# Two sigmoid recurrences cut into five chains of 26 rows instead of four of 32

## The chip, the cores and the metric

The kernel runs on one core of a Trainium2 chip. The metric is device time in microseconds (us) of one execution. A core has five engines that each work through their own queue of instructions in order and meet at semaphores: TensorE (PE in the profile, with PEld for its weight loads), VectorE (DVE), ScalarE (ACT), GpSimd (POOL) and SyncE (SP), which here issues the DMA transfers.

## The reference

The input `x` has shape (4, 32, 128, 128). Two layers follow each other; each is a convolution block with a residual, then a feed-forward block with a residual. The feed-forward block is what the change touches, and it stands in the program twice (`f0` after the first convolution block, `f1` at the end):

```python
def _L0_ffn_ref(x, W, V, gamma, beta):
    Wx = jnp.einsum('bti,hi->bth', x, W)
    # normalised over the whole batch, per feature
    Wx = ((flat - mean) * rsqrt(var + BN_EPS) * gamma + beta).reshape(B, T, H)
    def step(yt, wx_t):
        yt = sigmoid(wx_t + yt @ V.T)
        return (yt, yt)
    _, ys = scan(step, zeros((B, H)), swapaxes(Wx, 0, 1))
    return swapaxes(ys, 0, 1)
```

The scan runs over 4096 tokens (32 images of 128 rows) for each of 4 batch entries, and each step needs the one before it. A step is one 128 x 128 matrix product, an add and a sigmoid over 128 features.

## The kernel before

**How the recurrence is made parallel.** A sigmoid step shrinks differences fast, so the kernel doesn't start at the first token. It cuts the long scan into many short ones: each starts from a guess of 0.5 and takes `WARM = 12` steps on the tokens ahead of its own before its results count. The 128 columns of one step are the 4 batch entries times the 32 images, which run side by side; the 128 rows of an image are split among `QS = 4` chains of `LEN = 32` rows. One pass over all chains, one row each, is called a round here. So a recurrence is 12 warm-up rounds and then 32 rounds whose results count, 44 rounds of 4 steps. At the end `check` compares what each chain started from with what the chain before it ended with (tolerance `TOL`), and a flag `redo` starts a slow sequential version of everything if they differ.

**One step** (`step`, L1907 to L1913) is three instructions on three engines: a matmul of the weights with the chain's last state into a PSUM bank (L1910, two weight loads and two matmul passes in the trace[...]), on VectorE the scaled input row added in place in that bank (L1911, a SCALAR_TENSOR_TENSOR of 128x128), and on ScalarE the sigmoid from the bank into SBUF (L1912). Each chain has its own PSUM bank, with one buffer. The chains don't depend on each other, so while one is on VectorE another can be on TensorE.

**First recurrence** (`f0.scan()`, L1971). The sigmoid writes its result over the input row in `WX`. Nothing else runs on these engines meanwhile. After it come the 32 images of the second convolution block in an order written out by hand (`CONVOLUTIONS`, L54), which ends by filling `WX` and the statistics for the second recurrence; `f0.check()` is one piece of that list (`CK`).

**Second recurrence** (`f1.scan(output)`, L2252). While it warms up, SyncE's DMAs bring the residual rows back from DRAM into `XA`, turned so that partitions hold tokens (L2230). In the counting rounds, `output(i, ys)` (L2237) is called after each round for the row before: four transposes on TensorE into one PSUM bank `ps_out` (L2244, `ps_t` has two buffers), one VectorE add of that bank and `XA` into `res` (L2245, 128x512), and every second row four DMAs of `res` to the output (L2249), issued by SyncE.

**What sets the order.** The order of instructions on each engine is fixed when the kernel is built, and queues run in order. In the built program, a counting round of the second recurrence has four steps with the four transposes among them on TensorE, four adds L1911 and then the add L2245 on VectorE, and four sigmoids on ScalarE. After the last row VectorE runs `check` (L1953 to L1958), TensorE and VectorE make the flag (L2258 to L2262), all engines read it (L2289) and the program ends.

Of the kernel before, what the change touches and what calls it, by code (L numbers as in the profile page):

```python
# [40 lines left out]
GAIN = float(np.float32(np.sqrt(2.0)))  # L41


LEN, WARM = 32, 12
QS = P // LEN
TOL = 4e-6

FILTER_TOL = 4e-7
# [226 lines left out]
def _network(  # L275
# [14 lines left out]
    nc = tc.nc  # L290
    mm = nc.tensor.matmul
    tt = nc.vector.tensor_tensor
# [9 lines left out]
    XA = keep.tile([P, NB, NT, P], F32, name="XA")  # L302
# [7 lines left out]
    ident = keep.tile([P, P], F32, name="ident")  # L310
# [257 lines left out]
    H = 32  # L568
# [227 lines left out]
    with (  # L796
# [168 lines left out]
        p = big("ps_s4")[:, :NB]  # L965
# [47 lines left out]
        p = big("ps_pt").rearrange("p (g n) -> p g n", g=4)  # L1013
# [17 lines left out]
        for b in range(NB):  # L1031
            q = slice(32 * b, 32 * b + 32)
# [242 lines left out]
    with (  # L1275
# [3 lines left out]
        ys = [psy.tile([P, 8, 2 * KW], F32, name=f"ps_y{k}") for k in range(4)]  # L1279
        for g in range(4):  # L1280
            for x_ in range(2):
# [4 lines left out]
                for b in range(NB):  # L1286
                    t = dfp.tile([P, 2, KH * KW], F32, name="df")
# [7 lines left out]
                for k in range(4):  # L1295
# [29 lines left out]
    with (  # L1325
# [356 lines left out]
        with in_order():  # L1682
            for piece in MIXERS.split():
                name, c = piece.split(".")
# [176 lines left out]
    def parallel():  # L1861
# [13 lines left out]
        turned = ctx.enter_context(tc.tile_pool(name="turned", bufs=1, space=bass.MemoryType.DRAM)).tile(  # L1875
            [NT * NB, P, P], F32, name="turned")
# [4 lines left out]
        class Recurrence(Inputs):  # L1881
# [8 lines left out]
            def scan(self, after=None):  # L1890

                mv = xtp.tile([P, 2], F32, name=f"mv{self.layer}")
                nc.vector.bn_aggr(mv, self.stats.rearrange("p t s -> p (t s)"))
                s = xtp.tile([P, 2], F32, name=f"bs{self.layer}")
                rsqrt(s[:, 0:1], mv[:, 1:2], 1e-5, 1)
                tt(s[:, 0:1], s[:, 0:1], self.gamma, ALU.mult)
                stt(s[:, 1:2], mv[:, 0:1], -1.0, s[:, 0:1], ALU.mult, ALU.mult)
                tt(s[:, 1:2], s[:, 1:2], self.beta, ALU.add)

                G = rest[:, 1024 : 1024 + QS * P].rearrange("p (q n) -> p q n", q=QS)  # L1900
                nc.gpsimd.memset(G[:, 0, 0:NB], 0.0)
                last = xtp.tile([P, NT * NB], F32, name="last")
                ys = {}
                with tc.tile_pool(name="ps_s", bufs=1, space=PSUM) as ps_s:

                    def step(q, dst, prev, h):

                        p = ps_s.tile([P, 512], F32, tag=f"s{q}", name=f"ps_scan{q}")[:, :P]
                        p4 = p.rearrange("p (o n) -> p o n", o=4)
                        mm(p4, self.t[:, 1, :], prev, start=True, stop=True)  # L1910
                        stt(p4, WX[:, :, h, :], s[:, 0:1], p4, ALU.mult, ALU.add)  # L1911
                        nc.scalar.activation(dst, p4, AF.Sigmoid, bias=s[:, 1:2])  # L1912
                        return dst  # L1913

                    def tokens(v):
                        return v.rearrange("p (o n) -> p o n", o=4)

                    prev = [tokens(guess)] * QS
                    for k in range(WARM):
                        for q in range(QS):  # L1920

                            if k == WARM - 1:
                                dst = G[:, q] if q else last
                            else:
                                dst = wk.tile([P, NT * NB], F32, tag=f"yw{q}", name=f"yw{q}")
                            prev[q] = step(q, tokens(dst), prev[q], (q * LEN - WARM + k) % P)
                    nc.vector.tensor_copy(G[:, 0, NB:], last[:, : (NT - 1) * NB])
                    prev[0] = tokens(G[:, 0])
                    for i in range(LEN):
                        for q in range(QS):  # L1930
                            h = q * LEN + i
                            if after is None:
                                y = WX[:, :, h, :]
                            else:
                                y = wk.tile([P, NT * NB], F32, tag=f"y{q}", name=f"y{q}")
                                ys[q, i] = y
                                y = tokens(y)
                            prev[q] = step(q, y, prev[q], h)
                        if after is not None and i > 0:
                            after(i - 1, [ys.pop((q, i - 1)) for q in range(QS)])  # L1940
                    if after is not None:
                        after(LEN - 1, [ys.pop((q, LEN - 1)) for q in range(QS)])
                self.ends = last, G, prev

            def check(self):
# [32 lines left out]
        with (  # L1978
# [8 lines left out]
            norm, stats, held, ps_y = {}, {}, {}, {}  # L1987
# [234 lines left out]
            for piece in CONVOLUTIONS.split():  # L2222
# [3 lines left out]
                name = piece.rstrip("0123456789.")  # L2226
                work[name](*map(int, piece[len(name) :].split(".")))

        for i in range(0, LEN, 4):
            nc.sync.dma_start(XA[:, :, i : i + 4, :], turned.rearrange("n (q i) w -> n q i w", q=QS)[:, :, i : i + 4, :])  # L2230
        with (
            tc.tile_pool(name="outp", bufs=3) as outp,
            tc.tile_pool(name="ps_t", bufs=2, space=PSUM) as ps_t,
        ):
            res = None

            def output(i, ys):  # L2237

                nonlocal res
# [5 lines left out]
                tt(res[:, :, i % 2, :], XA[:, :, i, :], p, ALU.add)  # L2245
                if i % 2 == 1:
                    for q in range(QS):
# [125 lines left out]
```

## Time and profile before

| | us |
|---|---|
| time, median of 3 runs (lowest, highest) | 929.68 (929.39, 932.43) |
| the profiled execution, its own time | 931.59 |
| its span in the profile | 929.8 |
| first recurrence, from its first add L1911 to its last sigmoid | 489.06 to about 549 |
| second recurrence, warm-up, from its first add L1911 | 849.42 to 866.7 |
| second recurrence, counting rounds, to the last add L2245 | 866.7 to 919.98 |
| flag made, in the span | 923.36 |
| TensorE, VectorE, ScalarE, GpSimd busy over the span | 826.4, 736.1, 642.4, 324.9 |

The span is what lies between the first and the last instruction of the profile; the time has some start and end around it. In the profile's tables "busy" is the time in which an engine has an instruction under way, "mean ns" the length of one such instruction; instructions of one engine overlap a little, so the distance from one start to the next is shorter than the length. An entry in square brackets in the timeline is how long the engine sat idle before the row, and which instruction ended the wait. PEclk is the share of TensorE's full clock that was granted.

### The profile page before, as it was taken

What the parts mean: (1) busy time and instruction counts of PE and PEld (TensorE: products, weight loads), DVE (VectorE), ACT (ScalarE), POOL (GpSimd) and SP (SyncE); (2) the same over time, 40 slices, a digit from 0 to 9 for tenths busy, and PEclk for the clock granted to TensorE, in tenths of its full rate; (3) what the DMA queues carried; (4) which work ended last, traced back from release to release, by engine and by line L of the source; (5) the groups of instructions that cost most, each with busy time, mean ns of one, the idle gap of its engine ahead of it and who ended that gap; (6) DMA issues with size and microseconds to landing.
All of it is one profiled execution on the core that took longest, in us unless ns stands there. A gap on an engine that the chain in (4) does not pass through costs nothing.

```text
span 929.8 us, 30873 instructions
## 1 busy us (share of the span) xinstructions
PE 826.4 (89%) x12630; PEld 617.1 (66%) x12630; DVE 736.1 (79%) x2332; ACT 642.4 (69%) x1580; POOL 324.9 (35%) x537
## 2 busy tenths in 40 slices
PE   2999979997797889999778989999999999898995
PEld 1656556577564545565337877998888788785884
DVE  5997477777658989989888888896687677677996
ACT  2774636566764878998778855677777677786763
POOL 2000000002144455274410003797596686760000
PEclk9999979997767999999999998999999999998998
DMA  9905000000101111102100000111110101118443
GB/s 228 231 4 122 1 1 1 1 1 1 47 1 47 47 46 48 42 14 61 46 0 1 1 1 4 38 38 38 38 38 27 38 26 38 37 38 293 156 164 131
DMA packets 69080, 49.64 MB, mean 53 GB/s; under 512 B 4481, under 2 KB 63873, under 8 KB 68865
## 3 DMA queue, kind: packets, MB, share of 16 engines
q1 hardware_dynamic: 68593, 47.31, 17.9%
q8 instruction: 101, 1.65, 0.7%
q0 software_dynamic: 288, 0.01, 0.2%
q10 hardware_dynamic: 48, 0.26, 0.2%
q14 instruction: 50, 0.41, 0.1%
HBM read 30.68 MB, written 16.88 MB: 51 GB/s over the span
## 4 chain that ended last, share of the span: by engine, by line
PE 49%; DVE 23%; POOL 7%; ACT 5%; issue 3%; DVEq 0%; ACTq 0%; SPq 0%; POOLq 0%
PE ps_scan L1910 9%; PE ps_k L2062 5%; PE ps_d L2179 5%; DVE XA L1582 4%; DVE XA L1581 3%; PE ps_r L2062 3%; PE ps_y L2062 3%; PE ps_y L1301 3%; POOL XN L2041 3%; PE pm L1053 2%; PE ps_e L2186 2%; PE ps_w L2125 2%; PE ps_inv L479 2%; PE ps_st L1424 2%; PE ps_x L2062 2%
## 5 line engine op out<-in xcount | busy, mean ns | idle before, releaser
L1911 DVE SCALAR_TENSOR_TENSOR ps_scan<-WXY,bs,ps_scan 128x128 f32<-128x128 f32 x352 | 102.8, 352 | 10.5 <-PE ps_scan L1910 7.6
L2169 DVE SCALAR_TENSOR_TENSOR U<-raw 128x512 f32<-128x512 f32 x128 | 88.6, 712 | 22.8 <-ACT raw L2161 18.9
L2161 ACT COPY raw<-ps_k 128x512 f32<-128x512 f32 x128 | 72.4, 592 | 36.2 <-PE ps_k L2062 29.2
L2062 PE MATMUL ps_k<-WXY,q 64*64 64x134 f32 x2048 | 85.5, 284 | 1.2 <-DVE XA L2091 1.0
L2041 POOL TENSOR_SCALAR XN<-XA,c_r,c_o 128x128 f32<-128x128 f32 x120 | 75.0, 636 | 4.8 <-PE ps_r L2062 1.9
L2179 PEld LDWEIGHTS ps_d<-WXY,U 128*64 128x64 f32 x2048 | 65.9, 137 | 13.3 <-issue 8.7
L2179 PE MATMUL ps_d<-WXY,U 128*64 128x67 f32 x2048 | 73.3, 225 | 0.0
L2062 PEld LDWEIGHTS ps_k<-WXY,q 64*64 64x64 f32 x2048 | 59.7, 136 | 12.2 <-PE ps_e L2186 2.4
L2062 PE MATMUL ps_r<-WXY,XN 64*64 64x134 f32 x1024 | 57.4, 288 | 4.4 <-POOL XN L2041 3.0
L2041 POOL TENSOR_SCALAR xn<-XA,f_r,f_o 128x128 f32<-128x128 f32 x90 | 52.7, 594 | 15.0 <-PE ps_x L2062 8.7
L848 PE MATMUL ps_st<-cst,XA 128*128 128x130 f32 x256 | 43.7, 310 | 14.7 <-ACT XA L831 11.5
L1639 ACT ACTIVATE xn<-XA,f_o,f_r 128x128 f32<-128x128 f32 x120 | 51.0, 490 | 4.7 <-DVE f_o L1621 4.7
L848 PEld LDWEIGHTS ps_st<-cst,XA 128*128 128x128 f32 x256 | 35.4, 207 | 27.8 <-ACT XA L831 12.7
L1418 ACT ACTIVATE Z<-Z,k,aB 128x128 f32<-128x128 f32 x128 | 51.1, 481 | 3.4 <-DVE Z L1413 3.2
L1581 DVE SCALAR_TENSOR_TENSOR XA<-ps_inv,r1B,xin 128x128 f32<-128x128 f32 x128 | 44.1, 345 | 8.8 <-PE ps_inv L1574 8.8
L1582 DVE SCALAR_TENSOR_TENSOR XA<-Z,gB,XA 128x128 f32<-128x128 f32 x128 | 46.5, 363 | 5.0
L2147 ACT COPY q<-ps_r 128x512 f32<-128x512 f32 x64 | 37.8, 591 | 17.3 <-PE ps_r L2062 17.1
L1912 ACT ACTIVATE y<-ps_scan,bs 128x128 f32<-128x128 f32 x128 | 36.9, 363 | 15.2 <-DVE ps_scan L1911 15.0
L1910 PE MATMUL ps_scan<-y,wvt 128*128 128x128 f32 x248 | 45.8, 288 | 1.1
L494 PE MATMUL ps_inv<-invq,cst 64*128 64x512 f32 x128 | 41.9, 685 | 4.6 <-ACT invq L485 3.9
L2021 POOL TENSOR_TENSOR c_r<-c_e,neg_half 128x16 f32<-128x16 f32 (+2 forms) x10 | 24.8, 2483 | 57.2 <-DVE c_e L2014 57.2
L2062 PE MATMUL ps_y<-ident,WXY 64*64 64x64 f32 x1024 | 42.2, 282 | 2.6 <-DVE XA L2091 1.8
(452 smaller groups left out, 2229.6 us busy)
## 6 DMA issues: line engine op xcount, KB each, us to landing
XA<-in_x_dram SPq DMA_DIRECT2D x16, 512.0 KB, 7.4
xin<-in_x_dram SPq DMA_DIRECT2D x32, 256.0 KB, 3.3
turned<-XA SPq DMA_DIRECT2D x32, 256.0 KB, 2.4
XA<-turned SPq DMA_DIRECT2D x8, 1024.0 KB, 9.1
out_dram<-res SPq DMA_DIRECT2D x64, 128.0 KB, 2.1
WXY<-dd SPq DMA_DIRECT2D x4, 544.0 KB, 11.2
WXY<-md SPq DMA_DIRECT2D x4, 144.0 KB, 5.2
WXY<-m1d SPq DMA_DIRECT2D x1, 544.0 KB, 11.5
```

The costliest lines, as they stand in the source:

```text
L848: mm(p[:, i, :], XA[:, b, t0 + j + i, :], cst[:, C_E : C_E + 130], start=True, stop=True)
L1418: nc.scalar.activation(z, z, AF.Gelu, bias=k1, scale=aB[:, j : j + 1])
L1581: stt(a, p2[c, b][:, i], r1B[:, j : j + 1], xin[c, b - b % 2][:, b % 2, i], ALU.mult, ALU.add)
L1582: stt(a, Z[c][:, b, i], gB[c][:, n : n + 1], a, ALU.mult, ALU.add)
L1639: nc.scalar.activation(t[:, dst, :], a, AF.Identity, bias=sh, scale=sc_)
L1910: mm(p4, self.t[:, 1, :], prev, start=True, stop=True)
L1911: stt(p4, WX[:, :, h, :], s[:, 0:1], p4, ALU.mult, ALU.add)
L2041: e.tensor_scalar(dst, src_, r, o, ALU.mult, ALU.add)
L2062: m = mm(dst, data, taps, start=(n == 0 and (i, j) not in last), stop=(n == 1), skip_group_check=True)
L2161: nc.scalar.copy(raw[u, k], banks["k", u][:, k])
L2169: stt(U[u][:, k].rearrange("p k s m -> p (k s m)"), v, SLOPE, v, ALU.mult, ALU.max)
L2179: mm(p[HALVES[s], m, b, REACH[k]], U[v][:, b, k, s, HALVES[m]], DR[:, k, REACH[k]], start=(m == 0 and b == 0 and k == 0), stop=(k == 1), s ...
```

## The change

`LEN` becomes 26, so `QS` is 5: four chains of 26 rows and a last one of `SHORT = 24`. Both recurrences then have 12 + 26 = 38 rounds instead of 44; 36 of them have five steps, and the last two have four. Each chain still has a PSUM bank of its own, so the recurrence holds five. `f0.check()` and `f1.check()` compare five boundaries.

The output of the second recurrence is cut differently. The four long chains still share one bank `ps_out` for each row, but VectorE now adds two of its four parts (128x256). The other two parts are copied by ScalarE into SBUF (`held`) and added to `XA` by GpSimd (128x256). The fifth chain has a bank of its own, `ps_l`, with one buffer, which collects two rows; then ScalarE copies it and GpSimd adds it. The number of output DMAs stays 64 (13 pairs of rows times 4, and 12 of the fifth chain). The loads of `XA` become 13 DMAs instead of 8, with the same bytes.

```diff
-LEN, WARM = 32, 12
-QS = P // LEN
+LEN, WARM = 26, 12
+QS = -(-P // LEN)
+SHORT = P - (QS - 1) * LEN
...
                     for i in range(LEN):
                         for q in range(QS):
+                            if i >= (LEN if q < QS - 1 else SHORT):
+                                continue
                             h = q * LEN + i
...
                         if after is not None and i > 0:
-                            after(i - 1, [ys.pop((q, i - 1)) for q in range(QS)])
+                            after(i - 1, ys)
...
+        rows = XA.rearrange("p b t w -> p (b t) w")
+        even, odd = rows[:, : (QS - 1) * LEN, :], rows[:, (QS - 1) * LEN :, :]
         for i in range(0, LEN, 4):
-            nc.sync.dma_start(XA[:, :, i : i + 4, :], turned.rearrange("n (q i) w -> n q i w", q=QS)[:, :, i : i + 4, :])
+            n = min(4, LEN - i)
+            nc.sync.dma_start(even.rearrange("p (q i) w -> p q i w", i=LEN)[:, :, i : i + n, :],
+                              turned[:, : (QS - 1) * LEN, :].rearrange("n (q i) w -> n q i w", i=LEN)[:, :, i : i + n, :])
+            if i < SHORT:
+                nc.sync.dma_start(odd[:, i : i + 4, :], turned[:, (QS - 1) * LEN + i : (QS - 1) * LEN + i + 4, :])
         with (
             tc.tile_pool(name="outp", bufs=3) as outp,
             tc.tile_pool(name="ps_t", bufs=2, space=PSUM) as ps_t,
+            tc.tile_pool(name="ps_l", bufs=1, space=PSUM) as ps_l,
         ):
-            res = None
+            res = res_l = p_l = None
+            H = (QS - 1) // 2
+
+            def by_scalar(dst, a, p):
+                held = outp.tile([P, H, P], F32, tag="held", name="held")
+                nc.scalar.copy(held, p)
+                nc.gpsimd.tensor_tensor(dst, a, held, ALU.add)
 
             def output(i, ys):
...
-                    res = outp.tile([P, QS, 2, P], F32, name="res")
-                p = ps_t.tile([P, QS, P], F32, tag="t", name="ps_out")
-                for q in range(QS):
-                    nc.tensor.transpose(p[:, q, :], ys[q], ident)
-                tt(res[:, :, i % 2, :], XA[:, :, i, :], p, ALU.add)
+                    res = outp.tile([P, QS - 1, 2, P], F32, tag="res", name="res")
+                p = ps_t.tile([P, QS - 1, P], F32, tag="t", name="ps_out")
+                for q in range(QS - 1):
+                    nc.tensor.transpose(p[:, q, :], ys.pop((q, i)), ident)
+                a = even.rearrange("p (q i) w -> p q i w", i=LEN)[:, :, i, :]
+                tt(res[:, :H, i % 2, :], a[:, :H], p[:, :H], ALU.add)
+                by_scalar(res[:, H:, i % 2, :], a[:, H:], p[:, H:])
...
+                if i < SHORT:
+                    if i % 2 == 0:
+                        p_l = ps_l.tile([P, 2, P], F32, tag="l", name="ps_outl")
+                    nc.tensor.transpose(p_l[:, i % 2, :], ys.pop((QS - 1, i)), ident)
+                    if i % 2 == 1:
+                        res_l = outp.tile([P, 2, P], F32, tag="resl", name="resl")
+                        by_scalar(res_l, odd[:, i - 1 : i + 1, :], p_l)
+                        h = (QS - 1) * LEN + i - 1
+                        nc.sync.dma_start(out[:, :, h : h + 2, :].rearrange("b t h w -> t b (h w)"),
+                                          res_l.rearrange("p h w -> p (h w)"))
```

In the built program of the changed kernel the instructions between the two recurrences stand in the same order as before, except for `f0.check`'s larger operands and the place of the first matmuls around each recurrence. In the second recurrence's counting rounds ScalarE has five sigmoids, then the copy of `ps_out`, then in every second round the copy of `ps_l`. The copy of `ps_out` waits on a semaphore of VectorE.

More of the change, by code (lines that the diff above doesn't have):

```diff
@@ L1939, in scan @@
                         if after is not None and i > 0:
-                            after(i - 1, [ys.pop((q, i - 1)) for q in range(QS)])
+                            after(i - 1, ys)
                     if after is not None:
-                        after(LEN - 1, [ys.pop((q, LEN - 1)) for q in range(QS)])
+                        after(LEN - 1, ys)
                 self.ends = last, G, prev
@@ L2233, in parallel @@
             tc.tile_pool(name="ps_t", bufs=2, space=PSUM) as ps_t,
+            tc.tile_pool(name="ps_l", bufs=1, space=PSUM) as ps_l,
         ):
-            res = None
+            res = res_l = p_l = None
[4 more added lines that the diff above has]
+                nc.gpsimd.tensor_tensor(dst, a, held, ALU.add)
             def output(i, ys):
-                nonlocal res
+                nonlocal res, res_l, p_l
                 if i % 2 == 0:
-                    res = outp.tile([P, QS, 2, P], F32, name="res")
-                p = ps_t.tile([P, QS, P], F32, tag="t", name="ps_out")
-                for q in range(QS):
-                    nc.tensor.transpose(p[:, q, :], ys[q], ident)
-                tt(res[:, :, i % 2, :], XA[:, :, i, :], p, ALU.add)
+                    res = outp.tile([P, QS - 1, 2, P], F32, tag="res", name="res")
[5 more added lines that the diff above has]
+                by_scalar(res[:, H:, i % 2, :], a[:, H:], p[:, H:])
                 if i % 2 == 1:
-                    for q in range(QS):
+                    for q in range(QS - 1):
                         h = q * LEN + i - 1
```

## The prediction

> **What bounds the kernel now.** I read the two recurrences first as stretches of busy time, then their timelines, round by round. The four stretches are the first recurrence's warm-up and counting rounds, then the second's (columns: PE, PEld, DVE, ACT, POOL busy, PEclk, DMA share, GB/s):
>
> ```profile
> 489.06:505.30 16.24, 15.25 (x88) 13.38 (x88) 14.44 (x49) 14.30 (x45) 0.00 (x0) 0.89 0.00 1
> 505.30:548.90 43.60, 40.86 (x258) 34.55 (x257) 37.17 (x131) 37.50 (x132) 0.10 (x1) 1.00 0.00 1
> 849.40:866.20 16.80, 15.68 (x89) 13.44 (x89) 14.83 (x50) 14.66 (x47) 0.00 (x0) 0.88 0.96 358
> 866.20:919.30 53.10, 51.92 (x384) 43.78 (x384) 52.72 (x163) 37.52 (x130) 0.00 (x0) 1.00 0.43 142
> ```
>
> Only in the last is VectorE full (52.72 of 53.10). In the second no engine is, and a round of its timeline says why:
>
> ```profile
> 543.17 1.08 PEld L1910 LDWEIGHTS ps_scan<-WXY,wvt 128*128 128x128 f32 x8 [0.26 <-ACT WXY L1912]
> 543.70 1.14 DVE L1911 SCALAR_TENSOR_TENSOR ps_scan<-WXY,bs,ps_scan 128x128 f32<-128x128 f32 x4 [0.20 <-PE ps_scan L1910]
> 544.09 1.15 ACT L1912 ACTIVATE WXY<-ps_scan,bs 128x128 f32<-128x128 f32 x4 [0.19 <-DVE ps_scan L1911]
> 544.50 1.08 PEld L1910 LDWEIGHTS ps_scan<-WXY,wvt 128*128 128x128 f32 x8 [0.26 <-ACT WXY L1912]
> ```
>
> Each engine does the four chains' work and then waits for the next. The round, 544.50 - 543.17 = 1.34 us (seven such rounds agree), is one chain's way round: 0.53 from weight load to add, 0.39 to sigmoid, 0.41 to the next weight load. It is a latency; the number of chains doesn't set it. In a counting round of the second recurrence:
>
> ```profile
> 872.70 0.68 DVE L2245 TENSOR_TENSOR res<-XA,ps_out 128x512 f32<-128x512 f32 x1
> ...
> 873.30 1.12 DVE L1911 SCALAR_TENSOR_TENSOR ps_scan<-WXY,bs,ps_scan 128x128 f32<-128x128 f32 x4
> ...
> 874.10 0.30 PEld L1910 LDWEIGHTS ps_scan<-y,wvt 128*128 128x128 f32 x2 [0.27 <-ACT y L1912]
> ...
> 874.34 0.68 DVE L2245 TENSOR_TENSOR res<-XA,ps_out 128x512 f32<-128x512 f32 x1
> ```
>
> VectorE never waits: 0.60 from the start of the 512-wide add to the next, four adds in 1.03 (0.258 each), 1.64 us a round.
>
> **What the Trainium skill says.** "PSUM — Partial Sum Buffer", section "PSUM bank collisions raise a hardware error": two engines must not touch one bank and partition quadrant together, reads against reads included, so they are kept apart by a dependency. The new `held` copy therefore waits for VectorE's add of the same bank. This trace shows the same, for two readers of `ps_wx`:
>
> ```profile
> L451 ACT COPY WXY<-ps_wx 128x512 f32<-128x512 f32 x28 | 16.3, 581 | 15.7 <-DVE bn L447 15.6
> ```
>
> "SBUF — State Buffer", section "SBUF: two separate sides": VectorE and GpSimd block each other if VectorE reads two SBUF inputs while GpSimd reads SBUF. VectorE's adds in the counting rounds read one SBUF and one PSUM input, so GpSimd's new adds shouldn't slow them; in this trace GpSimd has nothing to do there (POOL x0), so no row shows it. "TensorE: Matmul & The Clock Gate", Part 1: after an idle window TensorE runs at half clock until it has been busy for about 3.4 us. The trace agrees: PEclk is 0.89 and 0.88 in the warm-ups, which follow waits for the normalisation, and 1.00 in the counting rounds.
>
> **Part 1: fewer rounds in the first recurrence.** Six of 44 rounds go: 6 x 1.34 = 8.0 us, if a round of five still takes 1.34. VectorE's distance between adds is at most (0.86 - 0.35) / 2 = 0.26 (row of three at 849.74, inputs ready), ScalarE's between sigmoids (1.15 - 0.37) / 3 = 0.26. Five take 1.30: just under 1.34, so the fifth chain fits in the idle 0.19 to 0.20 of DVE and ACT by overlapping the tail of one add with the head of the next. TensorE needs 0.11 a pass (weight loads at 873.13 and 873.47: two passes and one transpose in 0.34), 1.1 for five steps. Against that, the half clock: 11% of clock lost over 16.24 us is 3.6 us at half clock, where a pass costs 0.22 and TensorE bounds. Four steps take 1.77, five 2.2; 3.6 us then hold 1.63 rounds instead of 2.03, and 0.4 x 1.34 = 0.5 us is given back. Part 1: **-7.5 us**.
>
> **Part 2: the second recurrence.** Warm-up keeps 12 rounds. Its half clock lasts 24% of 16.8 = 4.0 us: 2.26 rounds against 1.82, 0.44 x 1.34 = 0.6 back. In the counting rounds, a full round of five costs each engine, start to start:
> - VectorE: five adds at 0.258 and a 256-wide add. The same shape takes 0.42 in L2202 on DVE; less the 0.08 of overlap that the 512-wide one has (0.68 - 0.60), 0.34. Sum 1.63.
> - TensorE: five steps of two passes and five transposes: 15 x 0.11 = 1.66.
> - ScalarE: five sigmoids at 0.255 (1.28) and a 256-wide copy. L1669's four copies of that shape take 1.21 with 0.39 each, so (1.21 - 0.39) / 3 = 0.27. Every second round has another for `ps_l`: 1.28 + 0.27 + 0.135 = 1.68. In front of the first copy ScalarE waits for VectorE's add: the add starts 0.26 after the last stt and ends 0.42 later, with 0.04 to pass it on; ScalarE is free 0.39 + 0.26 = 0.65 after that stt. The wait is 0.07. Queued behind it are the next round's sigmoids, and behind them TensorE's next steps. With it 1.75.
> - GpSimd: 1.5 adds a round at 0.73 (median of L2202 on POOL, 723 to 1204 ns) is 1.1: cover 0.6. SyncE: five DMAs in two rounds at 0.60 are 3.0 of 3.4: fits, nearly full. Neither gives back anything while a round is over 1.5.
>
> Three engines are within 0.1 of each other and their queues are in order, so the true round is not the largest sum but near it. The copies of odd rounds delay the first sigmoid of the next by about 0.3, and TensorE makes up half of it in the even round. I take 1.73, between ScalarE's sum with and without the wait. Before, first add to first add of the last round is 917.35 - 866.69 = 50.7 (31 rounds). Now 25: the first two as now (1.34 and 2.0, where transposes and adds start), 22 x 1.73 = 38.1, one with four chains at 1.4: 42.8. Gain 7.9. At the end VectorE compares five boundaries: one 0.20 more (920.10 to 920.30), and three operations of 640 instead of 512 columns at 0.13 more each, less 0.26 for the narrower last add: +0.3. The last GpSimd add and two DMAs end about 0.04 + 0.4 + 0.73 + 1.3 = 2.5 after VectorE's last add, and the flag takes 3.4 now (923.36 - 919.98), so they are hidden. Part 2: **-7.9 + 0.6 + 0.3 = -7.0 us**.
>
> **Part 3: what else moves.** `f0.check` costs VectorE 0.6 to 0.8 more amid the convolutions, where it is busy to 70 or 80%: 0 to 0.8 us, I take 0.4. The 13 loads of `XA` have the same bytes; about 16 us of issuing on SyncE end before the first output DMA (871.8), and the last landed near 866 in the warm-up's DMA share. The second load touches images 30 and 31, which are read until 841.8, while the first is still being issued (14.9 us for eight): nothing. Two or four extra matmuls from the guess lie ahead of the first add, which waits for the statistics: nothing; uncovered it would be 0.22 to 0.44.
>
> **Sum.** -7.5 - 7.0 + 0.4 = -14.1 us. The profiled execution took 931.59, so 917.5 by its own time; it lies 1.9 above the median of the runs, and from 929.68 I get **915.6 us**.
>
> **Rivals.**
> - A, the counting rounds lock worse: one round of 1.95, if each odd round's double copy delays the whole ring (TensorE's transposes, VectorE's 256-wide add, then the copy again) with no catching up. For it: three nearly full in-order engines; against: the sums' 1.63 to 1.75. 22 x 0.22 = 4.8 worse: 920.4.
> - B, five chains don't fit 1.34: VectorE or ScalarE needs 0.30 from one waiting instruction to the next, and the round is 1.50. For it: only 0.04 of slack. Against: 0.26 already holds with a wait before each. 36 rounds of five in the first and 12 in the second, each 0.16 longer: 7.7 worse, 923.3.
> - C, the output stage reaches the bound and the clock recovers as fast: rounds of 1.65 and no half-clock loss: 22 x 0.08 + 1.1 = 2.9 better, 912.7.
> - D, slower: TensorE falls to half clock in the counting rounds. A pass is 0.22 then and a round 15 x 0.22 = 3.3, 1.57 longer. From 9 such rounds (14.1 / 1.57), some 30 us at half clock, the change is a loss; with all 24 it is 953. Against: PEclk is 1.00 over these 53 us now, with fewer matmuls per us.
> - E, the change doesn't do what it says: a boundary fails the tolerance and the sequential version runs, more than doubling the time. Twelve warm-up steps are as before, so 0.01.
>
> **Chances and range.** A measurement tells 0.3% (2.8 us) from no change. The main case with C's side of it, 912 to 918.5, has 0.70; A 0.14; B 0.09; D and E 0.04; the rest, a gain eaten to within 0.3% by something unseen, 0.03. Eight in ten lie from 911.8, a little under C, to 921.5, which takes in A. Faster 0.93, same 0.03, slower 0.04.
>
> **What the profile after would show.** Rounds of 1.34 in the first recurrence with five adds each, DVE over 95% busy there; about 52 us instead of 59.9 from 489 to the first transpose. Counting rounds that alternate around 1.73, ACT waiting a little for `res`, and three engines over 90%. PEclk 1.00 there. GpSimd's new adds at 0.73. If those adds take 1.2, or SyncE's issues 0.7, POOL or SP bounds, and the round is 1.8 or more; if the sigmoids show idle time before `held` beyond 0.1, the wait for VectorE's add was priced too low.

## The result, and the profile after

The changed kernel takes 917.89 us (median of 4 runs, 913.69 to 918.55) where the kernel before took 930.28 beside it: a ratio of 0.9851, 95% interval [0.9821, 0.9881]. A second set of runs, on another occasion, gave 916.78 against 930.75, 0.987 [0.9851, 0.9889]. (The quotients of the medians are 0.9867 and 0.9850.) The prediction was 915.6 us, or 0.9848 of the median of 929.68 it was made from, with a range from 911.8 to 921.5.

The trace says where the time went. Both kernels were profiled twice, the second time in the runs e9 and e10 below. Stretches are cut at the starts of VectorE's adds (L1911 before, L1912 after); all in us:

| stretch | before | after | change | predicted |
|---|---|---|---|---|
| start to the first recurrence's first add | 489.06, 489.12 | 485.86, 487.19 | -3.2, -1.9 | 0 |
| first recurrence, first add to that of the last round | 58.65, 58.63 | 50.60, 50.60 | -8.0 | -7.5 |
| from there to the second recurrence's first add | 301.71, 301.59 | 301.95, 302.26 | +0.2, +0.7 | +0.4 |
| its warm-up | 17.27, 17.27 | 16.42, 16.42 | -0.9 | +0.6 |
| its counting rounds, first add to that of the last round | 50.66, 50.62 | 42.93, 42.94 | -7.7 | -7.9 |
| from there to the flag | 6.02, 6.07 | 7.18, 7.18 | +1.2, +1.1 | +0.3 |
| flag to the end of the span | 6.43, 6.37 | 6.97, 6.75 | +0.5, +0.4 | 0 |
| span | 929.8, 929.7 | 911.9, 913.3 | -17.9, -16.4 | -14.1 |

Without its first row the table sums to -14.7 and -14.4, against -14.1 predicted. The first row is work that the change doesn't touch; the first profile of the changed kernel, 913.69, is also the fastest of its runs, and the medians differ by 12.4 and 14.0.

The four stretches of busy time in the changed kernel (columns as in the prediction: PE, PEld, DVE, ACT, POOL busy, PEclk, DMA share, GB/s):

```profile
485.86:502.27 16.41, 15.43 (x114) 15.20 (x115) 16.34 (x63) 15.91 (x60) 0.00 (x0) 1.00 0.01 1
502.27:537.50 35.23, 34.70 (x254) 33.53 (x253) 34.48 (x128) 34.34 (x128) 0.10 (x1) 1.00 0.00 1
838.40:854.80 16.40, 15.40 (x114) 15.14 (x114) 16.34 (x63) 15.90 (x60) 0.00 (x0) 1.00 0.93 337
854.80:900.30 45.50, 45.10 (x382) 42.95 (x381) 45.11 (x157) 44.59 (x166) 25.98 (x37) 1.00 0.48 160
```

In the second and the fourth row TensorE, VectorE and ScalarE are all busy for over 97% of the stretch. Before, VectorE and ScalarE stood at 85 and 86% in the second row (37.17 and 37.50 of 43.60), and ScalarE at 71% in the fourth (37.52 of 53.10). And PEclk is 1.00 in both warm-ups, where it was 0.89 and 0.88: in this execution no half clock fell there.

Some 43 us into the first recurrence, in its counting rounds, with all engines:

```profile
529.21 2.25 DVE L1912 SCALAR_TENSOR_TENSOR ps_scan<-WXY,bs,ps_scan 128x128 f32<-128x128 f32 x8
529.26 2.21 PE L1911 MATMUL ps_scan<-WXY,wvt 128*128 128x128 f32 x15
529.34 2.21 ACT L1913 ACTIVATE WXY<-ps_scan,bs 128x128 f32<-128x128 f32 x8
529.35 1.93 PEld L1911 LDWEIGHTS ps_scan<-WXY,wvt 128*128 128x128 f32 x14
```

The gaps of 0.19 to 0.26 that each engine had per round are gone: eight adds follow one another in 2.25 us. The starts of the adds repeat every 1.34 us per round of five, in 33 of the 37 intervals. Five steps fit into the time of four, since that time was one chain's way round.

Two counting rounds, VectorE and ScalarE in order of time:

```profile
880.33 0.41 DVE L2262 TENSOR_TENSOR res<-XA,ps_out 128x256 f32<-128x256 f32 x1
...
880.66 1.52 DVE L1912 SCALAR_TENSOR_TENSOR ps_scan<-WXY,bs,ps_scan 128x128 f32<-128x128 f32 x5
...
880.82 0.37 ACT L2250 COPY held<-ps_out 128x256 f32<-128x256 f32 x1
...
881.09 0.38 ACT L2250 COPY held<-ps_outl 128x256 f32<-128x256 f32 x1
...
881.36 1.41 ACT L1913 ACTIVATE y<-ps_scan,bs 128x128 f32<-128x128 f32 x5
...
882.09 0.42 DVE L2262 TENSOR_TENSOR res<-XA,ps_out 128x256 f32<-128x256 f32 x1
...
882.43 1.38 DVE L1912 SCALAR_TENSOR_TENSOR ps_scan<-WXY,bs,ps_scan 128x128 f32<-128x128 f32 x5
```

From the one 256-wide add to the next it is 882.09 - 880.33 = 1.76 here; the distances from round to round of the adds L1912 settle into 1.62, 1.87, 1.62, 1.78 and again, 1.72 on average. The 1.87 and the 1.78 follow the rows whose output ScalarE copies twice: the five sigmoids can't start before 881.36.

The timeline at the end of the changed kernel, VectorE and GpSimd (start, length, then the instruction; a row with x3 holds three in succession):

```profile
898.96 0.73 POOL L2251 TENSOR_TENSOR resl<-XA,held 128x256 f32<-128x256 f32 x1
...
899.39 0.46 DVE L1956 TENSOR_TENSOR d<-last,y 128x128 f32<-128x128 f32 x1
...
899.77 0.28 DVE L1958 TENSOR_TENSOR d<-WXY,y 128x128 f32<-128x128 f32 x1
899.97 0.41 DVE L2262 TENSOR_TENSOR res<-XA,ps_out 128x256 f32<-128x256 f32 x1
900.01 0.72 POOL L2251 TENSOR_TENSOR res<-XA,held 128x256 f32<-128x256 f32 x1 [0.31 <-ACT held L2250]
900.30 1.51 DVE L1958 TENSOR_TENSOR d<-WXY,y 128x128 f32<-128x128 f32 x3
...
900.91 0.75 POOL L2251 TENSOR_TENSOR res<-XA,held 128x256 f32<-128x256 f32 x1 [0.18 <-ACT held L2250]
901.84 0.82 DVE L1959 TENSOR_TENSOR d<-d 128x640 f32<-128x640 f32 x1
```

And VectorE at the same place of the kernel before, where GpSimd has nothing to do:

```profile
918.98 0.28 DVE L1953 TENSOR_TENSOR d<-last,y 128x128 f32<-128x128 f32 x1
919.29 0.69 DVE L2245 TENSOR_TENSOR res<-XA,ps_out 128x512 f32<-128x512 f32 x1
919.89 0.69 DVE L1955 TENSOR_TENSOR d<-WXY,y 128x128 f32<-128x128 f32 x3
920.62 0.69 DVE L1956 TENSOR_TENSOR d<-d 128x512 f32<-128x512 f32 x1
```

Before, three subtractions of the comparison took 0.69 us. After, three take 1.51, and a fourth 0.46 instead of 0.28. One by one they are 577, 277 and 805 ns, and 455. The three long ones end at 899.843, 900.876 and 901.809; GpSimd's adds that run beside them, and that started before them, end at 899.694, 900.729 and 901.659, each 0.147 to 0.150 earlier. This is what the prediction hadn't priced.

### The profile page after: what moved, and what is told of

The parts are those of the page before. It is cut to its first block, busy times and chain, and to the rows that moved or that the text cites. A ratio compares the mean times of both kernels' runs of the same rounds, so it can differ in the third digit from the quotient of the medians.

```text
span 911.9 us, 31186 instructions
## 1 busy us (share of the span) xinstructions
PE 810.4 (89%) x12678; PEld 615.0 (67%) x12678; DVE 730.6 (80%) x2352; ACT 649.5 (71%) x1642; POOL 350.7 (38%) x575
## 4 chain that ended last, share of the span: by engine, by line
PE 43%; DVE 23%; ACT 10%; POOL 8%; issue 3%; DVEq 0%; ACTq 0%; POOLq 0%; SPq 0%
PE ps_k L2065 6%; PE ps_d L2182 5%; DVE XA L1583 4%; PE ps_scan L1911 4%; DVE XA L1582 4%; ACT WXY L1913 3%; ACT yw L1913 3%; PE ps_r L2065 3%; PE ps_y L1302 3%; PE ps_y L2065 3%; POOL XN L2044 2%; PE pm L1054 2%; PE ps_e L2189 2%; PE ps_st L1425 2%; PE ps_w L2128 2%
## 5 line engine op out<-in xcount | busy, mean ns | idle before, releaser
L1912 DVE SCALAR_TENSOR_TENSOR ps_scan<-WXY,bs,ps_scan 128x128 f32<-128x128 f32 x376 | 104.8, 351 | 1.3 <-PE ps_scan L1911 0.8
L2182 PEld LDWEIGHTS ps_d<-WXY,U 128*64 128x64 f32 x2048 | 66.8, 138 | 13.5 <-issue 8.7
L2044 POOL TENSOR_SCALAR xn<-XA,f_r,f_o 128x128 f32<-128x128 f32 x90 | 50.3, 567 | 15.6 <-PE ps_x L2065 9.1
L2150 ACT COPY q<-ps_r 128x512 f32<-128x512 f32 x64 | 37.8, 591 | 16.7 <-PE ps_r L2065 16.4
L2024 POOL TENSOR_TENSOR c_r<-c_e,neg_half 128x16 f32<-128x16 f32 (+2 forms) x10 | 24.8, 2481 | 49.6 <-DVE c_e L2017 49.6
L2195 ACT COPY q<-ps_d 128x512 f32<-128x512 f32 x64 | 38.1, 596 | 7.1 <-PE ps_d L2182 6.4
L1289 DVE TENSOR_TENSOR df<-WXY 128x1088 f32<-128x1088 f32 x32 | 40.2, 1286 | 2.1 <-PE ps_y L1302 2.0
```

Of the source, the lines that this page charges most:

```text
L2044: e.tensor_scalar(dst, src_, r, o, ALU.mult, ALU.add)
L2182: mm(p[HALVES[s], m, b, REACH[k]], U[v][:, b, k, s, HALVES[m]], DR[:, k, REACH[k]], start=(m == 0 and b == 0 and k == 0), stop=(k == 1), s ...
```

## The experiments

**What each half of the change is worth.** The first run has five chains in the first recurrence alone, the second run in the second recurrence alone, with the new output. The third has both, but VectorE adds the whole output as before; the fourth has the new split of the output on four chains.

The first run's edit of the kernel before (`chains` works out the three values from a length; the second run has `LENS = 32, LEN` in the changed kernel, where `LEN` is 26):

```diff
+LENS = 26, LEN
...
+LEN, QS, SHORT = chains(LEN)
...
             def scan(self, after=None):
+                LEN, QS, SHORT = chains(LENS[self.layer])
```

> Only the first recurrence has five chains of 26; the second keeps four of 32 and VectorE's 128x512 adds. Theory (each recurrence gains by itself; a round of the first is a latency of 1.34 us whether four or five chains share it): 6 x 1.34 = 8.0 us less, its span from first to last add 58.6 before and 50.6 now, the time about 0.991 of the kernel before. Rival 1 (most of the gain lies in the second recurrence, the first having given part back at half clock): 5 us or less, 0.995. Rival 2 (the split of the output's adds earns the whole gain): no change here, 1.000.

Measured: 924.0 us, ratio 0.9922 [0.9907, 0.9936]. The first recurrence took 51.93 us; two rounds at its start, at half clock, took 2.19 and 1.78. The second recurrence's counting rounds were 50.56, the end 6.04 to the flag, both as before.

> Only the second recurrence has five chains and the divided output; the first keeps four of 32. Theory: 26 counting rounds of 1.72 instead of 32 of 1.63, 8.6 us less from first to last add, about 1.2 given back in the end stretch: 7.4 less, 0.992 of the kernel before. Rival 1 (the gain is in the second recurrence): 9 or more, 0.990 or lower. Rival 2 says the same as the theory here.

Measured: 924.7 us, ratio 0.9933 [0.992, 0.9947]. Counting rounds 42.83, first recurrence 59.29. From the last round's first add to the flag it took 7.55 us, so the longer end belongs to this half. The two halves give -7.1 and -6.4 us; their sum, -13.5, is what the whole change gave within the intervals.

```diff
-                tt(res[:, :H, i % 2, :], a[:, :H], p[:, :H], ALU.add)
-                by_scalar(res[:, H:, i % 2, :], a[:, H:], p[:, H:])
+                tt(res[:, :, i % 2, :], a, p, ALU.add)
...
-                        by_scalar(res_l, odd[:, i - 1 : i + 1, :], p_l)
+                        tt(res_l, odd[:, i - 1 : i + 1, :], p_l, ALU.add)
```

> The changed kernel, but VectorE does all of the output's adds again (128x512 each row, and 128x256 every second row for the fifth chain); nothing of them on ScalarE or GpSimd. Theory (VectorE is the bound then): a full counting round is 5 x 0.258 + 0.60 + 0.34 / 2 = 2.06 us, 0.34 longer than in the changed kernel; 24 of them give 8 back, so the second recurrence gains nothing by five chains alone; about 0.9935 of the kernel before with the first recurrence's 8 us less, and a shorter end stretch by up to 1. Rival 2: the whole gain is lost, 1.000. Rival 3 (TensorE or the in-order coupling sets the counting round anyway): at most 2 lost, 0.987.

Measured: 925.42 us, ratio 0.994 [0.9925, 0.9954]. VectorE in two counting rounds of this run:

```profile
879.96 0.42 DVE L2274 TENSOR_TENSOR resl<-XA,ps_outl 128x256 f32<-128x256 f32 x1
880.29 1.39 DVE L1912 SCALAR_TENSOR_TENSOR ps_scan<-WXY,bs,ps_scan 128x128 f32<-128x128 f32 x5
881.58 0.69 DVE L2262 TENSOR_TENSOR res<-XA,ps_out 128x512 f32<-128x512 f32 x1
882.18 1.39 DVE L1912 SCALAR_TENSOR_TENSOR ps_scan<-WXY,bs,ps_scan 128x128 f32<-128x128 f32 x5
```

VectorE has no gap and the rounds are 1.89 and 2.22; the counting stretch is 50.91, as long as with four chains (50.66), and GpSimd has nothing to do. Where VectorE bounds, the number of adds counts, and it is the same however many chains share them. Five chains gain nothing in the counting rounds by themselves. In this run, with GpSimd idle, the end took 6.58 instead of 7.18.

The fourth run has five chains in the first recurrence and four in the second, with the two halves of `ps_out` split as in the change:

```diff
-                tt(res[:, :, i % 2, :], XA[:, :, i, :], p, ALU.add)
+                tt(res[:, :H, i % 2, :], XA[:, :H, i, :], p[:, :H], ALU.add)
+                by_scalar(res[:, H:, i % 2, :], XA[:, H:, i, :], p[:, H:])
```

> The changed kernel, but the second recurrence has four chains of 32 again, with the output's adds divided between VectorE and ScalarE with GpSimd. Theory: VectorE needs 4 x 0.258 + 0.34 = 1.37 a round, TensorE 12 x 0.11 = 1.32, ScalarE 4 x 0.255 + 0.27 + 0.07 = 1.36, one chain's way round 1.34, and ScalarE's copy stands in front of the next sigmoids; so 1.40 to 1.50, 31 of them 43.4 to 46.5 where the changed kernel has 42.9. The split alone earns 4 to 7 of the 7.8 us of the counting rounds, and five chains the rest: 0.985 to 0.989 of the kernel before. Rival 3 (five chains earn it, the split is needed only to carry them): 1.60 a round, 0.992.

Measured: 922.93 us, ratio 0.9916 [0.9902, 0.993]. The counting stretch was 46.58, and its busy time (columns as above):

```profile
859.24:905.82 46.58, 45.99 (x370) 41.89 (x370) 46.23 (x154) 45.26 (x154) 21.07 (x29) 1.00 0.47 156
```

So the split alone took 4.0 us from the counting rounds and five chains alone nothing, while together they took 7.7. The time shows less of it. Its ratio is the rival's 0.992 and not the 0.985 to 0.989 expected; it is the stretch, 0.1 above the expected end against the 49.6 of the rival's rounds of 1.60, that speaks for the theory. Against the first run, which has the same five chains in its first recurrence, the time is 1.1 us lower. Of the 4.0 us, 0.5 went in the profile to the way to the flag, and 2.5 to the stretch from the flag to the end (8.78 against 6.32). That last stretch is 6.3 to 7.3 in eleven of the other profiles shown here and 9.43 in one, that of the eighth run. In these two the extra lies in one place: GpSimd stands for 2.38 and 2.47 us between two of its last instructions, where no other profile has more than 0.1, and the other engines wait for it. Why it stands there is not shown.

**Is 1.34 us a latency, and where does VectorE take over?** Six chains of 22 rows in the first recurrence:

```diff
-QS = -(-P // LEN)
-SHORT = P - (QS - 1) * LEN
+LENS = 22, LEN
...
+LEN, QS, SHORT = chains(LEN)
```

> First recurrence in six chains of 22 rows (the last has 18), the second as in the changed kernel. Theory: a round of up to five chains is a latency of 1.34 us, and beyond that VectorE's adds bound it, 0.258 us each: 6 x 0.258 = 1.55. From the first add to the first add of the last round: 30 rounds of six at 1.55 and 3 of five at 1.34, 50.5 us, against 50.6 in the changed kernel; the whole run within 1 us of the changed one (917 to 919). Rival (five did not reach VectorE's bound, its adds can be packed closer than 0.258 us): the round stays at 1.34, the stretch is 44.2, and the run is 6.4 us faster, about 911.5. If six chains overfill a queue and the ring locks worse, the round is 1.7 or more and the run is 4 us or more slower.

Measured: 917.14 us, ratio 0.9854 [0.9837, 0.987], the same as five chains within the intervals. Rounds of six take 1.55 or 1.56 in 25 of 30 intervals, as 6 x 0.258 gives. The stretch is 52.66 instead of 50.5: half clock at its start (rounds of 1.85 and 2.44) and the seam between warm-up and counting rounds (1.68 and 2.28) make the difference. VectorE's row in this run:

```profile
519.82 4.48 DVE L1920 SCALAR_TENSOR_TENSOR ps_scan<-WXY,bs,ps_scan 128x128 f32<-128x128 f32 x17
```

Seventeen adds without a gap. ScalarE's sigmoids follow one another after 0.258 as well in these rounds; at their own 0.255 six of them make 1.53, so this run separates VectorE from ScalarE by 0.02 us only. TensorE, with 12 passes of 0.11, is not the bound. Five chains, 1.30 us of adds in a way round of 1.34, are at the point where the bound changes hands, and a sixth chain removes rounds and lengthens them by the same amount.

**What lengthens the end.** In this kernel VectorE adds the whole 128x512 of the last two rows, and GpSimd has nothing to do when the comparison runs:

```diff
-                tt(res[:, :H, i % 2, :], a[:, :H], p[:, :H], ALU.add)
-                by_scalar(res[:, H:, i % 2, :], a[:, H:], p[:, H:])
+                if i < SHORT:
+                    tt(res[:, :H, i % 2, :], a[:, :H], p[:, :H], ALU.add)
+                    by_scalar(res[:, H:, i % 2, :], a[:, H:], p[:, H:])
+                else:
+                    tt(res[:, :, i % 2, :], a, p, ALU.add)
```

> The changed kernel, except that VectorE adds the whole 128x512 of the last two rows, without ScalarE and GpSimd. Theory (at the end GpSimd's last two adds and the comparison's subtractions on VectorE, which read two SBUF inputs, block each other): the stretched subtractions (455, 577 and 805 ns) come back to 276 to 290 ns, and from the first add of the last round to the flag it takes 7.18 - 0.17 - 0.29 - 0.52 + 0.26 for the wider last add = 6.4 to 6.5 us; the counting rounds stay at 42.9; the run is 0.8 us faster than the changed kernel. Rival (the subtractions are stretched by the DMA traffic or by five boundaries as such): they stay at 450 to 800 ns, and the flag comes 7.2 to 7.5 us after that add.

Measured: 916.66 us, ratio 0.9852 [0.9835, 0.9868]. The same kernel ran once more beside the changed kernel:

> The kernel in which VectorE adds all of the last two rows, once more and beside the changed kernel on the same chip. From its first run: 6.8 us from the last round's first add to the flag against 7.2 to 7.5, so 0.4 to 0.7 us faster than the changed kernel, if the time shows so little; subtractions of 0.28 us. If it is not faster, the gain stays in the trace alone.

Measured: 917.95 us, ratio 0.9878 [0.9862, 0.9893], beside 916.78 for the changed kernel. So the time shows no gain. A gain of this size could hardly show in it: the second warm-up alone, at half clock in both profiles of this kernel and not in those of the changed kernel, took 17.89 and 18.05 us against 16.42. The trace does show it, in both profiles; VectorE and GpSimd at the end of the second:

```profile
903.27 0.72 POOL L2251 TENSOR_TENSOR resl<-XA,held 128x256 f32<-128x256 f32 x1
903.35 0.69 DVE L2266 TENSOR_TENSOR res<-XA,ps_out 128x512 f32<-128x512 f32 x1
903.96 0.28 DVE L1956 TENSOR_TENSOR d<-last,y 128x128 f32<-128x128 f32 x1
904.25 0.69 DVE L2266 TENSOR_TENSOR res<-XA,ps_out 128x512 f32<-128x512 f32 x1
904.85 0.89 DVE L1958 TENSOR_TENSOR d<-WXY,y 128x128 f32<-128x128 f32 x4
```

Four subtractions take 0.89 and the one before them 0.28, although the same five boundaries are compared and SyncE's output transfers still run. To the flag it is 6.81 instead of 7.18. That is not the 6.4 to 6.5 expected: I had counted one wider add, and there are two after the last round's first add (903.35 and 904.25), 0.26 each. And I had counted the first subtraction's 0.18, which is not on the way to the flag: in the run without the fifth chain's last rows, below, it takes 282 ns, and the flag comes after 7.18 all the same. So about 0.8 was to be saved and 0.5 lost, and 0.37 shows. The rival, that transfers or the five boundaries stretch the subtractions, is out.

**Which engine sets a counting round.** Here ScalarE's copy, GpSimd's add and the DMA of the fifth chain are made for its first two rows only; the other 22 rows of its output are left out, while TensorE's transposes stay.

```diff
-                    if i % 2 == 1:
+                    if i == 1:
```

> The changed kernel, but ScalarE's copy, GpSimd's add and the output DMA of the fifth chain are made for its first two rows only; its other 22 rows of the output are left out, their transposes stay. Theory 1 (ScalarE's second copy in every second round holds up the next sigmoids, as the prediction had it): rounds repeat at 1.64 to 1.67, TensorE's and VectorE's sums, the counting stretch is 25 rounds with about 41.2 us against 42.93, and ScalarE is busy 5% less of it. Theory 2 (TensorE with 15 passes of 0.11 us and VectorE set the round, and the 1.78 to 1.87 come from the transposes and the 256-wide add): the alternation stays, mean 1.70 to 1.73, 42.5 to 43 us.

Measured: 915.84 us, ratio 0.9841 [0.9825, 0.9858]; the counting stretch 42.02, rounds of 1.65 and 1.71. ScalarE in two rounds:

```profile
880.35 0.37 ACT L2250 COPY held<-ps_out 128x256 f32<-128x256 f32 x1
880.62 1.40 ACT L1913 ACTIVATE y<-ps_scan,bs 128x128 f32<-128x128 f32 x5
882.07 0.37 ACT L2250 COPY held<-ps_out 128x256 f32<-128x256 f32 x1
882.34 1.40 ACT L1913 ACTIVATE y<-ps_scan,bs 128x128 f32<-128x128 f32 x5
```

Neither theory's number: 41.2 was one, 42.5 to 43 the other. The second copy, with the GpSimd add and the DMA that follow from it, costs 42.93 - 42.02 = 0.9 us in all, 0.085 for each pair of rounds, though the copy occupies ScalarE for 0.27. So the other engines absorb two thirds of it. TensorE's starts say what is left: its passes begin 0.111 apart, 1.66 for 15 of them, and the longer distances among them add 0.017 a round here and 0.060 in the changed kernel. The difference, 0.043, is all of what the edit saved, and 1.68 is TensorE with next to no waiting.

**Does SyncE's queue hold anything up?** In the changed kernel one issue follows another after 0.645 us, and five in a pair of rounds take 3.23 of 3.44. Here the fifth chain's output goes out every fourth row, on top of the edit for the last two rows:

```diff
+                    if i % 4 == 0:
+                        res_l = outp.tile([P, 4, P], F32, tag="resl", name="resl")
...
-                        res_l = outp.tile([P, 2, P], F32, tag="resl", name="resl")
...
-                        h = (QS - 1) * LEN + i - 1
...
+                    if i % 4 == 3:
+                        h = (QS - 1) * LEN + i - 3
```

> As the kernel in which VectorE adds all of the last two rows, and the fifth chain's output goes out every four rows by one DMA of 256 KB instead of every two rows by one of 128 KB: 58 output DMAs instead of 64. Theory (SyncE's issuing, 0.645 us from issue to issue and so 3.23 of 3.44 us in two rounds, is nearly full but bounds nothing, since three tiles of res absorb its stalls): the counting stretch stays at 42.9 (42.6 to 43.1), SyncE's last issue is about 3 us earlier than it was relative to the flag, and the run equals the one without this edit within 0.5 us. Rival (SyncE's stalls hold up the res tiles, seen as GpSimd's three waits of 2.6 us in all for output DMAs): the stretch falls by 0.5 to 2 us, to 41 to 42.4, and the run with it.

Measured: 918.06 us, ratio 0.9867 [0.9851, 0.9884]. Counting stretch 42.93, to the hundredth that of the changed kernel; 6.80 to the flag. SyncE doesn't set the round. The expected lead at the end did not come: its last issue ends at 905.91, 0.02 before the flag, where in the changed kernel it ends 0.12 after. Its last full group of eight issues took 6.75 us, where the earlier ones took 5.61 to 6.43, and that used up part of the lead; where the rest went is not shown. The time is not better, with a stretch from flag to end of 9.43 us in the profile.

**Both kernels once more.**

> The kernel before once more, unchanged, for a second profile of it. Theory (the 3.2 us by which the changed kernel's first recurrence starts earlier, 485.86 against 489.06, is a difference from run to run in code that did not change): the start of the first recurrence varies from profile to profile, here anywhere from 485.5 to 489.5, and only the stretches repeat: 58 to 59.5 from the first add to that of the last round, 50.5 to 50.8 in the counting rounds, 6.0 to 6.1 from the last round's first add to the flag. Rival (the change moves the start): 489.0 to 489.5 again.

Measured: ratio 1.0003 [0.9995, 1.0011]. The stretches repeat to 0.1 us (table), and so does the start of the first recurrence, 489.12. That is the rival's number.

> The changed kernel once more, unchanged, for a second profile and a narrower interval. Theory (the parts that the change touches give 8.05 + 7.7 less the 1.2 at the end, the rest varies): 916 to 918.5, ratio 0.984 to 0.987; its stretches repeat: 50.6 without and 51.9 with half clock in the first recurrence, 42.9 in the counting rounds, 7.2 to 7.5 to the flag; the subtractions at the end stretch again while GpSimd adds. If the subtractions are at 0.28 this time, the stretch was chance.

Measured: 916.78 us, ratio 0.987 [0.9851, 0.9889]. The stretches repeat to 0.01 us where no half clock falls, and the first recurrence starts at 487.19. Of the other kernels with five chains in the first recurrence some start it late, at 488.87, 489.44 and 489.13 (first, third and fourth run), some early, at 487.35 and 486.73 (seventh and eighth), and the sixth run's kernel does both, at 487.09 in its first profile and 488.59 in its second. Matched instruction by instruction with the kernel before, the lead of 1 to 3 us arises between 110 and 320 us, in the first convolution block, where the half-clock windows of TensorE fall differently. Nothing there was changed. One and the same program differs by 1.3 and by 1.5 us between its two profiles, so a good part of the lead comes from the run; whether the change adds to it stays open. In the profiles it is worth 0 to 3 us. The three subtractions stretched again, to 455, 581 and 806 ns, and each ended 0.148 to 0.150 after a GpSimd add.

## Why the prediction was right, and where it was not

- **Part 1, "1.34 is a latency; the fifth chain fits".** Right: rounds of five take 1.34, and those of six 1.55, so the price of 0.258 an add and the bound at five both hold (ScalarE, at 0.255, is as near to it). Rival B (1.50) is out. That the stretch shrank by just 6 x 1.34 = 8.0 is luck: the half clock that the profiles of the changed kernel escaped (0.7) makes up for a term that was missing (0.7, the seam below).
- **"0.5 us is given back" at half clock.** The mechanism was right and the size near, but it is not in the two profiles of the changed kernel. Where half clock fell into a first recurrence of five chains, in the first and third run, the stretch was 51.93 and 51.90 against 50.60, 1.3 more. The kernel before loses 0.7 to it (two rounds of 1.68 and 1.71). The difference is 0.6. The same in the second warm-up: 17.60 to 18.05 with half clock in six of the runs with five chains there, 16.42 without, and 17.27 in the kernel before with it, so 0.3 to 0.8 is given back; the prediction had 0.6. Why the changed kernel escapes it in both its profiles is not shown. One thing that the change does to it is visible: ahead of the first recurrence's first step TensorE's weight loads rest for 3.42 us in all three profiles with four chains there, and half clock follows in all three; in the nine with five chains they rest for 2.21 to 2.34 (the matmuls from the guess, which stood in part among the last ones before them, all come after those in the changed kernel), and half clock follows in two. No run tests whether the shorter rest is the reason.
- **Missing in part 1: the seam.** Between warm-up and counting rounds VectorE makes a copy of 0.22 us (L1928) and a chain changes its source. The three intervals there were 1.63, 1.34 and 1.34 with four chains and are 1.60, 1.53 and 1.89 with five, 0.7 longer. That the ring has hardly any idle time left to absorb the copy in is my reading of it; no run tests it. With half clock on both sides the gain is 58.63 - 51.92 = 6.7, which is 7.5 less the seam; without it on the one side, 8.0.
- **Part 2, "I take 1.73".** Measured 1.72, and 42.93 for the stretch of 42.8. The alternation came as described, and the seventh run shows its cause and size: with ScalarE's second copy and what hangs on it gone, 0.085 goes in two rounds, and of an alternation of 0.16 to 0.25 there remains 0.06. Of the engines' sums, VectorE's 1.63 and TensorE's 1.66 stand. So does the wait of the `held` copy for VectorE's add, priced at 0.07 a round. As idle time it shows once only, after the last round (0.53, before the copy at 900.46), because ScalarE's instructions overlap by 0.12. From start to start it is in the rounds too: the sigmoids follow each other after 0.25, the copy follows the last of them after 0.315 on average, and mostly 0.09 to 0.11 after the end of VectorE's add (880.74, and 880.82 for the copy). ScalarE's own work is 1.66 a round by these distances, and with 0.065 of waiting it gives the 1.72. TensorE comes to the same from its side, 1.66 and 0.06. GpSimd's adds take 0.727 (0.73 predicted). SyncE's issues take 0.645 apart, not 0.60, and bound nothing, as the eighth run shows.
- **"At the end ... +0.3": the step that failed.** It measured +1.2 and +1.1 to the flag. The 640-wide operations were right: from L1959 to the flag it takes 3.09 against 2.74. But L1959 itself starts 4.09 after the last round's first add, against 3.27 before, 0.8 later, where the forecast had one more subtraction (0.20) and a narrower add (-0.26), so nothing. What failed is "the last GpSimd add and two DMAs ... are hidden". The add does end in time (901.66, the flag is at 904.93), but while it and the two before it run they stop the comparison. The Trainium skill says it in the place I cited for the counting rounds, "SBUF — State Buffer", section "SBUF: two separate sides": of a VectorE operation with two SBUF inputs and a GpSimd operation, whichever starts first has the shared ports for its whole length and "the other fully blocks". I applied it to the adds that read PSUM, which are indeed not slowed (0.416 on average beside GpSimd's adds), and not to the subtractions, which read two tiles in SBUF. The trace agrees to the hundredth: six stretched subtractions in two profiles all end 0.147 to 0.150 after a GpSimd add, and so do eight in the second, fourth, fifth and seventh run (0.146 to 0.149). Together the three are 0.18 + 0.30 + 0.52 = 1.0 us longer, and the last two of them, 0.82, make up the 0.8. SyncE's last issue ends 0.12 after the flag and not well before it; what that costs is not shown.
- **Part 3.** The stretch between the recurrences grew by 0.24 and 0.67; 0.4 was taken. With other kernels it runs from 300.59 (fifth run, six boundaries in `f0.check`) to 302.92 (third), so a term of 0.4 can't be told from the differences between runs.
- **Rivals A, C, D, E.** Rounds of 1.95 or 1.65 didn't come, TensorE kept its full clock in the counting rounds (PEclk 1.00), and no boundary failed (the time would have more than doubled). Of C, its second half, no half-clock loss, did come in the profile.

That the total lies within 0.3% of the forecast owes something to errors of both signs. In the profile, the second warm-up came out 1.5 below the forecast and the first recurrence 0.5; the way to the flag came out 0.8 above it and the stretch behind the flag 0.5.

## What to carry to other kernels

Before chains are added to a ring of engines, compare the way round of one chain with the sum of the busiest engine's steps: up to where they meet (here five chains, 1.30 of 1.34) more chains lengthen no round, though they cost something at the seam (0.7 us here) and wherever half clock falls on them (0.6 more than with four chains), and beyond it they only trade rounds for length. Where one engine is already full, more chains do nothing until its load is moved, and moving the load alone gives only part of it (in the counting rounds 0 and 4.0 us alone, 7.7 together). When work goes to GpSimd, look through everything that VectorE does in the same microseconds, the few operations after the loop too, for those with two SBUF inputs.

## What was unexpected in the hardware

- A VectorE subtraction of 0.28 us with two SBUF inputs took up to 0.81 when it met a GpSimd add of 0.72 to 0.75 that had started first, and ended 0.15 after it. A 512-wide multiplication with both inputs in SBUF, 0.69 otherwise, took 1.09 in the fourth run and ended 0.55 after the GpSimd add. In both cases what came after GpSimd's end was about 0.14 us less than the instruction's usual length. VectorE's add with one PSUM input, beside the same GpSimd adds, kept its 0.42, and its 128-wide adds L1912 their 0.35 (85 of them beside a GpSimd add, 0.351 against 0.350).
- The stretch from the flag to the end of the program took 6.3 to 7.3 us in most profiles and 8.78 and 9.43 in two, with the same instructions. That is as much as a third of the second part's gain. In both the extra is GpSimd's, which stands for 2.4 to 2.5 us between two of its last instructions; why is not explained.
- One to three of the 64 output issues of SyncE take 1.3 to 2.2 us instead of 0.55 to 0.60 (both profiles of the changed kernel, the fourth run, and the kernel before, with 1.36 and 2.23). GpSimd waits three times for an output DMA, 2.6 us in all, and the round doesn't grow by it.
